# Projections and feed-forward products issued as four 32-column tiles

## The chip, the cores and the metric

The kernel runs on one core of a Trainium2 chip. The metric is the device time of one launch in microseconds. The page of the profile shows one execution of the program, taken by the hardware profiler; the times are those of separate runs.

## The reference

One layer of a graph transformer on x of shape (8, 2048, 256) in float32, with a 2048 x 2048 adjacency matrix as mask. F = 8 frames, N = 2048 rows, C = 256 channels, H = 8 heads of D = 32.

```
q, k, v = split(x @ w_qkv)                        # (F, N, 256) each, 8 heads of 32
attn    = softmax(where(adj > 0, q k^T / sqrt(32), -1e9))
x1      = layernorm(x + attn v) * g1 + be1
f       = relu(x1 @ w1 + b1) @ w2 + b2
x2      = layernorm(x1 + f) * g2 + be2
out     = layernorm(x + x2)
```

## The kernel before

All products are in float32. The main loop of `fast_path` runs over 1024 **items** (f, qc, g, mb): 8 frames, 4 chunks `qc` of 512 query rows, 2 groups `g` of 4 heads, 16 blocks `mb` of 128 key rows. Sixteen items with the same (f, qc, g) make one group of sums. An item does this:

- `scores` (L217, on TensorE, PE in the profile): four products k^T q, one per head, each from 32 partitions (contraction over 32 channels) to 128 rows by 512 columns. They use four row strips of the array side by side. They are issued two items ahead of their use (`LEAD = 2`), into three pairs of PSUM banks that rotate.
- L220 on VectorE (DVE) adds the mask to two heads at a time, from PSUM into an SBUF tile `p`; two of these per item.
- `exponentials` (L224 on ScalarE, ACT): one exponential over the four heads, 128 x 2048.
- `values` (L236): four products, one per head, v of 128 x 32 (stationary) with `p` of 128 x 512 (moving), each to 32 of the 128 PSUM partitions. They use four column strips of the array side by side.
- `add_up`: softmax denominators. The `p` tiles of sixteen items are summed partly by GpSimd (POOL, L258), partly by accumulating DMAs that GpSimd issues (L255).

Everything else is **fill**: generators that are advanced once per item, just ahead of the item's scores, by `advance`. Each has a due time. A generator yields `BANK` when it needs one of the two side PSUM banks, and at most one gets one per item; `MORE` splits a piece of PE work over two items where nothing else is late. So on PE the order is: values of item t, then one piece of fill (or none), then scores of item t+3, values of item t+1, and so on. The fill pieces on PE are:

- L174 in `channels`: a projection to q^T or k^T, two products (halves `a` of the 256 input channels) of a 128 x 128 weight block with x^T, 512 columns.
- L199 in `project`: the projection to v, 4 row blocks `j` times 2 halves `a`, x^T of 128 x 128 stationary, 128 columns of weights moving.
- L409 in `feed_forward`: as L174, with w1.
- L421 in `feed_forward`: 4 row blocks times 2 halves, h^T of 128 x 128 stationary, w2 of 256 columns moving.
- L294 in `denominator`: column sums with a 128 x 32 block of ones, four heads side by side in column strips, as the values.
- Transposes L151, L301, L330, L396, and L126 for the mask in the opening (`begin`).

ScalarE copies most of these pieces out of PSUM (L176, L202, L410); VectorE adds the output of L421 (L423), and takes the statistics of the norms (L265, L266). GpSimd finishes the norms and multiplies and adds the affine rows (L341, L343, L399, L401).

A float32 product appears in the trace as two weight loads (PEld, LDWEIGHTS) and two MATMUL records, so a piece of L174 with both halves, which is four records, is split by `MORE` into two pieces of two where it can be. The names PEld, PE, DVE, ACT, POOL and SP are those of the profile.

Of the kernel before, what the change touches and what calls it, by code (L numbers as in the profile page):

```python
# [19 lines left out]
P = 128  # L20
H = 8
D = 32
# [17 lines left out]
def stats(nc, small, t, mhalf):  # L40
    st = small.tile([P, nc.vector.BN_STATS_DIM], F32, name="st")
    nc.vector.bn_stats(st, t)
    mv = small.tile([P, nc.vector.BN_AGGR_DIM], F32, name="mv")
    nc.vector.bn_aggr(mv, st)
    rs = small.tile([P, 1], F32, name="rs")
    nc.gpsimd.tensor_scalar(rs, mv[:, 1:2], EPS, 1.0, op0=ALU.add, op1=ALU.mult)
    nc.gpsimd.tensor_tensor(rs, rs, mhalf, ALU.pow)
    return mv, rs


def normalize(nc, dst, t, mv, rs):
# [4 lines left out]
def fast_path(ctx, tc, cst, x, adj, out, RS):  # L56
    nc = tc.nc
    F, N, C = x.shape
# [20 lines left out]
    ident, identb, wqkv, w1s, w2s = cst["ident"], cst["identb"], cst["wqkv"], cst["w1s"], cst["w2s"]  # L79
# [7 lines left out]
    def bank(dt=F32):  # L87
        shape = [P, CH] if dt == F32 else [P, 2, CH]
        if state["side"] is not None:
            i = 1 - state["side"]  # L90
            return ps_x[i].tile(shape, dt, name=f"x{i}")
        i = state["turn"]
        state["turn"] = (i + 1) % 5
        pool = ps_s[i] if i < 3 else ps_x[i - 3]
        return pool.tile(shape, dt, name=f"s{i}" if i < 3 else f"x{i - 3}")
# [9 lines left out]
    def give(t):  # L105
        live[:] = [None if u is t else u for u in live]
# [35 lines left out]
    def queries(f, c, xT):  # L142
        for g in range(2):
            yield from channels(QT, qp, "qT", (f, c, g), xT, g * P)
# [23 lines left out]
    def channels(store, pool, name, key, xT, k0):  # L168
        yield BANK
        ps = bank()  # L170
        for a in range(2):
            if a:
                yield MORE
            nc.tensor.matmul(ps, wqkv[:, a, k0:k0 + P], xT[:, a, :], start=(a == 0), stop=(a == 1))  # L174
        store[key] = pool.tile([P, CH], F32, name=name)
        nc.scalar.copy(store[key], ps)  # L176

    def reload(f, c):
        while (f, c) not in XT:
            yield 1  # L180
        yield INPUTS - 1
        xT = take([P, 2, CH], F32)
        nc.sync.dma_start(xT, XD[f][c])
        yield 3
        return xT

    def project(f, c, g, xT=None):
        if xT is None:
            xT = yield from reload(f, c)
            while len(KT) < (2 * f + g) * NCK + c:  # L190
                yield 1
        yield from channels(KT, kp, "kT", (f, c, g), xT, C + g * P)
        yield BANK
        ps = bank()
        for j in range(TPC):
            if j == TPC // 2:
                yield MORE
            for a in range(2):
                nc.tensor.matmul(ps[:, j * P:(j + 1) * P], xT[:, a, j * P:(j + 1) * P],  # L199
                                 wqkv[:, a, 2 * C + g * P:2 * C + (g + 1) * P], start=(a == 0), stop=(a == 1))  # L200
        v = vp.tile([P, TPC, P], F32, name="v")
        nc.scalar.copy(v, ps.rearrange("p (j c) -> p j c", c=P))  # L202
        V[f, c, g] = v
        give(xT)
# [74 lines left out]
    def rows(v):  # L279
        return v[:, None, :].to_broadcast([P, TPC, C])  # L280
# [54 lines left out]
    def tail(f, qc, y, xin):  # L335
        yield from norm(y)
        yield from feed_forward(y)
        yield 1
        z = y
        yield from norm(z)  # L340
        nc.gpsimd.tensor_tensor(z, z, rows(cst["g2r"]), ALU.mult)  # L341
        yield 1
        nc.gpsimd.tensor_tensor(z, z, rows(cst["be2r"]), ALU.add)  # L343
        yield 1
        nc.gpsimd.dma_start(z, xin, accum_op=ALU.add)
        yield 7
        yield from norm(z)
        nc.sync.dma_start(out[f, qc * CH:(qc + 1) * CH, :].rearrange("(p j) c -> p j c", p=P), z)
        state["tails"] -= 1
# [20 lines left out]
    def finish(f, qc):  # L370
        y = yp.tile([P, TPC, C], F32, name="y")
        xr, xb = state["rows"], take([P, TPC, C], F32)
        yield from divide(f, qc, y)
        nc.vector.tensor_tensor(y, y, xr, ALU.add)
        norm_halves(y)
        nc.vector.tensor_tensor(xb, xr, rows(cst["be2r"]), ALU.add)
        yield from feed_forward(y)
        z = y
        norm_halves(z)
        for h in range(0, TPC, 2):  # L380
            nc.vector.tensor_tensor(z[:, h:h + 2], z[:, h:h + 2], rows(cst["g2r"])[:, h:h + 2], ALU.mult)
            nc.vector.tensor_tensor(z[:, h:h + 2], z[:, h:h + 2], xb[:, h:h + 2], ALU.add)
        norm_halves(z)
        dst = out[f, qc * CH:(qc + 1) * CH, :].rearrange("(p j) c -> p j c", p=P)
        for h in range(0, TPC, 2):
            nc.sync.dma_start(dst[:, h:h + 2], z[:, h:h + 2])

    def feed_forward(y):
        yield TURNED
        state["turned"] = True  # L390
        yT = work.tile([P, 2, CH], F32, name="turned")
        for a in range(2):
            yield BANK
            ps = bank()
            for j in range(TPC):
                nc.tensor.transpose(ps[:, j * P:(j + 1) * P], y[:, j, a * P:(a + 1) * P], ident)  # L396
            nc.scalar.activation(yT[:, a, :], ps, AF.Identity, bias=cst["be1c"][:, a:a + 1], scale=cst["g1c"][:, a:a + 1])
        yield 1
        nc.gpsimd.tensor_tensor(y, y, rows(cst["g1r"]), ALU.mult)  # L399
        yield 1  # L400
        nc.gpsimd.tensor_tensor(y, y, rows(cst["be1b2r"]), ALU.add)  # L401
        hT = work.tile([P, 2, CH], F32, name="hT")
        for d in range(2):
            yield BANK
            ps = bank()
            for a in range(2):
                if a:
                    yield MORE
                nc.tensor.matmul(ps, w1s[:, a, d * P:(d + 1) * P], yT[:, a, :], start=(a == 0), stop=(a == 1))  # L409
            nc.scalar.activation(hT[:, d, :], ps, AF.Relu, bias=cst["b1s"][:, d:d + 1], scale=1.0)  # L410
        state["turned"] = False
        yield 1
        z = y
        for jj in range(0, TPC, 2):
            yield BANK
            ps = bank()
            for j in range(jj, jj + 2):
                if j > jj:
                    yield MORE
                for d in range(2):  # L420
                    nc.tensor.matmul(ps[:, (j - jj) * C:(j - jj + 1) * C], hT[:, d, j * P:(j + 1) * P], w2s[:, d, :],  # L421
                                     start=(d == 0), stop=(d == 1))
            nc.vector.tensor_tensor(z[:, jj:jj + 2, :], ps.rearrange("p (b c) -> p b c", c=C), z[:, jj:jj + 2, :], ALU.add)  # L423


# [18 lines left out]
    def advance(t, free=True, finish=False):  # L444
# [18 lines left out]
        while state["holder"] and (finish or late and state["holder"][2] == MORE):  # L463
# [4 lines left out]


    NEXT = {(1, 1): [(turn, 0)], (3, 1): [(turn, 1)], (3, 10): [(project, 0, 0)], (5, 1): [(turn, 2)],  # L470
            (5, 8): [(project, 1, 0)], (6, 0): [(turn, 3)], (6, 4): [(project, 2, 0)], (6, 8): [(project, 3, 0)],
            (6, 12): [(project, 0, 1)], (7, 0): [(project, 1, 1)], (7, 4): [(project, 2, 1)], (7, 8): [(project, 3, 1)]}

    def begin():
# [91 lines left out]
def general_path(ctx, tc, cst, x, adj, out):  # L566
# [20 lines left out]
    with tc.For_i(0, F, 1) as f:  # L587
# [24 lines left out]
        with tc.For_i(0, N, P) as n0:  # L612
# [12 lines left out]
            for h in range(H):  # L625
# [27 lines left out]
                nc.vector.tensor_scalar(y[:, h * D:(h + 1) * D], o, rsum, None, op0=ALU.mult)  # L653
            nc.vector.tensor_tensor(y, y, xs, ALU.add)
            mv, rs = stats(nc, small, y, cst["mhalf"][:, 0:1])
            normalize(nc, y, y, mv, rs)
            nc.vector.tensor_tensor(y, y, cst["g1r"], ALU.mult)
# [17 lines left out]
            nc.vector.tensor_tensor(z, pf, y, ALU.add)  # L675
            nc.vector.tensor_tensor(z, z, cst["b2r"], ALU.add)
            mv, rs = stats(nc, small, z, cst["mhalf"][:, 0:1])
            normalize(nc, z, z, mv, rs)
            nc.vector.tensor_tensor(z, z, cst["g2r"], ALU.mult)
            nc.vector.tensor_tensor(z, z, cst["be2r"], ALU.add)  # L680
            nc.vector.tensor_tensor(z, z, xs, ALU.add)
            mv, rs = stats(nc, small, z, cst["mhalf"][:, 0:1])
            normalize(nc, z, z, mv, rs)
            nc.sync.dma_start(out[bass.ds(f, 1), bass.ds(n0, P), :].rearrange("o p c -> p (o c)"), z)
# [114 lines left out]
```

## Time and profile before

| | |
|---|---|
| median of 3 runs | 3441.08 us (3438.21 to 3442.04) |
| profiled execution, first to last instruction (span) | 3433.5 us |
| median less span | 7.6 us |
| PE busy | 3205.3 us, 22036 MATMUL records |
| DVE busy | 2736.9 us |
| ACT busy | 2427.4 us |
| POOL busy | 2588.2 us |
| DMA engines, 800 to 1300 us | busy 0.76 of the time |
| granted TensorE clock, mean | 0.985 |

The page gives the span of the profiled execution and what its engines did in it; its time as the runs are timed is not given, and the 7.6 us between the two rows is taken as what lies around the span. Busy time is the union of an engine's instructions, the mean of a group is that of one record, and records overlap on PE, where several products stream side by side. The start times of PE's records are what is read below: the distance from the first record of a piece to the first record of the next is what the piece costs.

### The profile page before, as it was taken

How to read it: one execution, taken by the hardware profiler on the slowest of the kernel's cores; microseconds unless marked ns; L12 is line 12 of the kernel's file. 1: busy time of each engine (PE TensorE's matmuls, PEld its weight loads, DVE VectorE, ACT ScalarE, POOL GpSimd, SP SyncE). 2: the span in 40 equal slices, each digit the busy share in tenths (PEclk: the TensorE clock that was granted, in tenths of full speed). 3: DMA queues.
4: the chain of work that ended last, by engine and by line, in shares of the span. 5: the costliest groups of instructions: out<-in, count | busy, mean ns of one | idle time of the engine just before them, and what ended most of it. 6: DMA issues, size and time to landing. Idle time of an engine off the chain costs nothing. (4 is left out here: it accounts for less than half of the span.)

```text
span 3433.5 us, 54404 instructions
## 1 busy us (share of the span) xinstructions
PE 3205.3 (93%) x22036; PEld 1035.0 (30%) x22036; DVE 2736.9 (80%) x3203; ACT 2427.4 (71%) x1937; POOL 2588.2 (75%) x1357
## 2 busy tenths in 40 slices
PE   7999999999999999999999999999999999999994
PEld 5222333223332333322332223322233223332222
DVE  4788877878778877888778788787878878788884
ACT  3677777767777767777767677777777767777773
POOL 0577778787777787888777787777777877787884
PEclk8999999999999999999999999999999999999997
DMA  8677778778678777778767778678787677777773
GB/s 308 149 158 166 180 167 185 149 153 198 151 171 171 161 169 176 160 164 184 174 151 173 158 165 193 147 160 174 165 184 164 149 170 178 169 168 154 153 154 85
DMA packets 149297, 575.98 MB, mean 168 GB/s; under 512 B 14608, under 2 KB 67344, under 8 KB 99888
## 3 DMA queue, kind: packets, MB, share of 16 engines
q0 software_dynamic: 64560, 435.85, 63.0%
q1 hardware_dynamic: 83664, 135.30, 11.7%
q8 instruction: 174, 2.85, 0.3%
q10 hardware_dynamic: 816, 1.31, 0.1%
q14 instruction: 83, 0.68, 0.1%
HBM read 131.99 MB, written 37.75 MB: 49 GB/s over the span
## 5 line engine op out<-in xcount | busy, mean ns | idle before, releaser
L220 DVE TENSOR_TENSOR p<-s,mask 128x1024 f32<-128x1024 f32 x2048 | 2409.3, 1218 | 561.6 <-PE s L217 326.4
L224 ACT ACTIVATE p<-p 128x2048 f32<-128x2048 f32 x1024 | 1956.0, 1910 | 535.4 <-DVE p L220 448.2
L258 POOL TENSOR_TENSOR p<-p 128x2048 f32<-128x2048 f32 x382 | 1815.1, 4755 | 311.1 <-ACT p L224 309.7
L217 PE MATMUL s<-qT,kT 32*128 32x512 f32 x8192 | 1174.4, 643 | 135.1 <-DVE p L220 129.6
L236 PE MATMUL x<-p,v 128*32 128x512 f32 x8192 | 1095.1, 607 | 2.4 <-ACT p L224 2.4
L255 POOL DMA_DIRECT2D p<-p x384 | 358.4, 989 | 426.0 <-DMA p<-p 201.6
L217 PEld LDWEIGHTS s<-qT,kT 32*128 32x128 f32 x8192 | 321.2, 183 | 741.8 <-DVE p L220 683.1
L236 PEld LDWEIGHTS x<-p,v 128*32 128x32 f32 x8192 | 161.4, 108 | 783.6 <-issue 282.1
L174 PE MATMUL x<-in,wqkv 128*128 128x512 f32 x472 | 257.3, 643 | 21.0 <-DMA in<-xd 17.2
L294 PE MATMUL x<-p,ones 128*32 128x512 f32 x2016 | 239.3, 592 | 0.0
L276 ACT ACTIVATE y<-y,nb,rs 128x256 f32<-128x256 f32 x372 | 219.3, 591 | 25.3 <-POOL nb L273 25.2
L265 DVE BATCH_NORM_STATS2 st<-y 128x6 f32<-128x256 f32 x372 | 154.9, 416 | 6.0 <-DMA y<-in_x_dram 6.0
L174 PEld LDWEIGHTS x<-in,wqkv 128*128 128x128 f32 x472 | 75.0, 191 | 206.1 <-issue 157.5
L421 PE MATMUL x<-w2s,hT 128*128 128x256 f32 x512 | 128.0, 392 | 0.0
L409 PE MATMUL x<-turned,w1s 128*128 128x512 f32 x248 | 127.3, 625 | 0.3 <-ACT hT L410 0.3
L296 ACT COPY dT<-x 128x512 f32<-128x512 f32 x63 | 36.9, 585 | 126.1 <-PE x L294 126.1
L199 PEld LDWEIGHTS x<-wqkv,in 128*128 128x128 f32 x896 | 105.8, 191 | 64.6 <-issue 35.2
L199 PE MATMUL x<-wqkv,in 128*128 128x128 f32 x896 | 120.5, 284 | 0.0
L421 PEld LDWEIGHTS x<-w2s,hT 128*128 128x128 f32 x512 | 91.9, 189 | 64.1 <-issue 50.8
L294 PEld LDWEIGHTS x<-p,ones 128*32 128x32 f32 x2016 | 65.5, 110 | 150.8 <-issue 150.2
L270 POOL TENSOR_TENSOR rs<-rs,mhalf 128x4 f32<-128x4 f32 x93 | 97.1, 1044 | 7.7
L176 ACT COPY kT<-x 128x512 f32<-128x512 f32 x59 | 34.5, 585 | 81.0 <-PE x L174 81.0
(117 smaller groups left out, 1433.5 us busy)
## 6 DMA issues: line engine op xcount, KB each, us to landing
p<-p POOLq DMA_DIRECT2D x384, 1024.0 KB, 10.4
mask<-md SPq DMA_DIRECT2D x248, 128.0 KB, 6.8
y<-in_x_dram POOLq DMA_DIRECT2D x62, 512.0 KB, 5.8
in<-xd SPq DMA_DIRECT2D x59, 512.0 KB, 10.2
p<-in_adj_dram SPq DMA_DIRECT2D x16, 1024.0 KB, 10.0
out_dram<-y SPq DMA_DIRECT2D x31, 512.0 KB, 3.0
in<-in_x_dram SPq DMA_DIRECT2D x29, 512.0 KB, 10.0
xd<-in SPq DMA_DIRECT2D x28, 512.0 KB, 7.6
```

Of the source, the lines that this page charges most:

```text
L174: nc.tensor.matmul(ps, wqkv[:, a, k0:k0 + P], xT[:, a, :], start=(a == 0), stop=(a == 1))
L199: nc.tensor.matmul(ps[:, j * P:(j + 1) * P], xT[:, a, j * P:(j + 1) * P], wqkv[:, a, 2 * C + g * P:2 * C + (g + 1) * P], start=(a == 0), s ...
L217: nc.tensor.matmul(ps2[half][:, j, :], KT[f, mb // TPC, g][r:r + D, (mb % TPC) * P:(mb % TPC + 1) * P], QT[f, qc, g][r:r + D, :], start=Tr ...
L220: nc.vector.tensor_tensor(pt[:, 2 * half:2 * half + 2, :], ps, MK[f, qc, mb // 2][:, mb % 2, None, :].to_broadcast([P, 2, CH]), ALU.add)
L224: nc.scalar.activation(PT[item], PT[item], AF.Exp, scale=1.0 / math.sqrt(D))
L236: nc.tensor.matmul(O[grp][r:r + D, :], V[f, mb // TPC, g][:, mb % TPC, r:r + D], PT[item][:, h, :], start=(mb == 0), stop=(mb == LAST))
L255: nc.gpsimd.dma_start(PT[f, qc, g, chain[0]], PT.pop(item), accum_op=ALU.add)
L258: nc.gpsimd.tensor_tensor(first, first, PT.pop(item), ALU.add)
L265: nc.vector.bn_stats(st, t[:, j, :])
L276: nc.scalar.activation(t[:, j, :], t[:, j, :], AF.Identity, bias=nb[:, j:j + 1], scale=rs[:, j:j + 1])
L294: nc.tensor.matmul(ps[r:r + D, :], cst["ones"], term[:, h, :], start=(n == 0), stop=(n == len(terms) - 1))
L421: nc.tensor.matmul(ps[:, (j - jj) * C:(j - jj + 1) * C], hT[:, d, j * P:(j + 1) * P], w2s[:, d, :], start=(d == 0), stop=(d == 1))
```

## The change

A new helper issues one product as four, each with 32 columns of the stationary operand, to 32 of the output's partitions. The four products L174, L199, L409 and L421 go through it. Nothing else changes: the loops, the banks, the yields, the copies and the queues are as before, and no operand is laid out anew. The number of PE records for these four lines goes up fourfold. All lines below the helper move down by five.

```diff
+def in_columns(nc, out, lhsT, rhs, start, stop):
+    for r in range(0, P, D):
+        nc.tensor.matmul(out[r:r + D], lhsT[:, r:r + D], rhs, start=start, stop=stop)

 # channels
-            nc.tensor.matmul(ps, wqkv[:, a, k0:k0 + P], xT[:, a, :], start=(a == 0), stop=(a == 1))
+            in_columns(nc, ps, wqkv[:, a, k0:k0 + P], xT[:, a, :], start=(a == 0), stop=(a == 1))

 # project
-                nc.tensor.matmul(ps[:, j * P:(j + 1) * P], xT[:, a, j * P:(j + 1) * P],
-                                 wqkv[:, a, 2 * C + g * P:2 * C + (g + 1) * P], start=(a == 0), stop=(a == 1))
+                in_columns(nc, ps[:, j * P:(j + 1) * P], xT[:, a, j * P:(j + 1) * P],
+                           wqkv[:, a, 2 * C + g * P:2 * C + (g + 1) * P], start=(a == 0), stop=(a == 1))

 # feed_forward
-                nc.tensor.matmul(ps, w1s[:, a, d * P:(d + 1) * P], yT[:, a, :], start=(a == 0), stop=(a == 1))
+                in_columns(nc, ps, w1s[:, a, d * P:(d + 1) * P], yT[:, a, :], start=(a == 0), stop=(a == 1))
...
-                    nc.tensor.matmul(ps[:, (j - jj) * C:(j - jj + 1) * C], hT[:, d, j * P:(j + 1) * P], w2s[:, d, :],
-                                     start=(d == 0), stop=(d == 1))
+                    in_columns(nc, ps[:, (j - jj) * C:(j - jj + 1) * C], hT[:, d, j * P:(j + 1) * P], w2s[:, d, :],
+                               start=(d == 0), stop=(d == 1))
```

## The prediction

> **What bounds the kernel now.** First the busy shares of the page:
>
> ```profile
> PE 3205.3 (93%) x22036; PEld 1035.0 (30%) x22036; DVE 2736.9 (80%) x3203; ACT 2427.4 (71%) x1937; POOL 2588.2 (75%) x1357
> ```
>
> PE leads, but busy time on PE is modelled, so I read the distances between starts instead, in the timeline of PE. Two stretches of it (start, length, engine, line, tiles, count, and in brackets the idle time before it):
>
> ```profile
> 730.63 1.16 PE L199 MATMUL x<-wqkv,in 128*128 128x128 f32 x8
> 731.72 1.14 PE L217 MATMUL s<-qT,kT 32*128 32x512 f32 x8
> 732.79 1.06 PE L236 MATMUL x<-p,v 128*32 128x512 f32 x8
> ...
> 739.91 1.14 PE L217 MATMUL s<-qT,kT 32*128 32x512 f32 x8 [0.41 <-DVE p L220]
> 740.98 1.07 PE L236 MATMUL x<-p,v 128*32 128x512 f32 x8
> 742.45 1.14 PE L217 MATMUL s<-qT,kT 32*128 32x512 f32 x8 [0.41 <-DVE p L220]
> ```
> ```profile
> 800.80 1.06 PE L236 MATMUL x<-p,v 128*32 128x512 f32 x8
> 801.80 1.98 PE L409 MATMUL x<-turned,w1s 128*128 128x512 f32 x4
> 803.71 1.14 PE L217 MATMUL s<-qT,kT 32*128 32x512 f32 x8
> 804.78 1.06 PE L236 MATMUL x<-p,v 128*32 128x512 f32 x8
> 805.78 1.99 PE L421 MATMUL x<-w2s,hT 128*128 128x256 f32 x8
> 807.70 1.14 PE L217 MATMUL s<-qT,kT 32*128 32x512 f32 x8
> ...
> 812.76 1.07 PE L236 MATMUL x<-p,v 128*32 128x512 f32 x8
> 813.64 1.90 PE L294 MATMUL x<-p,ones 128*32 128x512 f32 x16
> 815.48 1.14 PE L217 MATMUL s<-qT,kT 32*128 32x512 f32 x8
> ```
>
> An item without fill takes 2.54 us (739.91 to 742.45): PE needs 2.07 and then waits 0.41 for the mask add of DVE, which has 2 x 1.22 us to do. DVE bounds it. An item with a piece of fill takes 3.1 us or more, with no wait on PE: PE bounds it. So a gain in the fill counts, as long as the item stays longer than DVE's and ACT's work in it. The list of waits says the same, with little waiting on PE in all:
>
> ```profile
> PE s L217 <- DVE p L220: 129.6, 276, 1.4
> PE x L174 <- DMA in<-xd: 17.2, 7, 3.4
> ```
>
> [...] Values to scores, or to any full-array piece, take 996 ns from start to start (median, all lines); values to L294, which has the values' tile shape, take 882. The drain is 114 ns. [...] after a change of mode, the second record of a full-array product starts 533 to 534 ns after the first and that of the values 454, which over 427 of streaming leaves 107 and 27. Inside one mode the load is hidden: two more records of L174 cost 858 ns (1914 less 1056). [...] Here four pairs of load and product start 6.7 ns apart. [...]
>
> **The change, piece by piece.** VectorE, ScalarE, GpSimd and the DMA queues keep their instructions and (bar a few at the end) their order; on PE no piece moves. L174, L199, L409 and L421 stream the same columns, in the values' mode instead of the full-array mode.
>
> Each piece follows values and precedes scores. Before: values 996 (with the drain), then the piece with its exposed load and drain. After: values 882, then the piece's stream, then a drain of 114 before the scores, as L294 shows it: 1830 for 16 records, 2 x 858 + 114.
>
> - L174, L409, 2 records: before 996 + 1056 = 2052. After 882 + 858 + 114 = 1854. **198 ns** less. With 4 records 858 more on both sides, so 198 again.
> - L199, 8 records: before 996 + 1088 = 2084; a record streams in 111.6 ns ((1981 - 1088) / 8). After 882 + 893 + 114 = 1889. **195 ns** less.
> - L421, 4 records: before 996 + 1060; 864 for four more. After 882 + 864 + 114. **196 ns** less.
>
> In the timeline of PE I count the periods from values to values with one of these: 191 of L174, 78 of L409, 77 of L199, 63 of L421. 269 x 0.198 + 140 x 0.195 = **80.6 us** off PE, all in items that PE bounds now.
>
> Not all of it reaches the end. In each of the 409 periods I took DVE's and ACT's busy time, plus 30 ns per instruction for the gap between two; the period cannot fall below either. Many periods of L174 hold norm statistics (0.42 + 0.18 us) besides the two mask adds, 3.03 us of DVE in a period of 3.12, so little is won there. Item by item 57 us are left (54 with a gap of 60 ns, 66 with none). Averaged over three items, where a late DVE catches up in the next, 72. I take 58: scores run only three half-items ahead, so little is lent, and POOL lends nothing (below).
>
> In the opening the pieces L174 and L199 stand between transposes, all in one mode now. Eight chunks get two changes of mode each: 114 + 27 into the strips, 114 + 107 back, 0.36 us a chunk, 2.9 us in all. PE runs without a gap from 36 to 55 us there, but afterwards waits for DVE's conversion of the adjacency matrix. I take 1.5 on the path; 0 and 2.9 are the ends.
>
> The new cost that the trace of before does not show is four times the records per streamed column: 8 (four loads, four products) for each 111.6 ns of L199, 14 ns a record; 27 ns for L421, 54 for L174 and L409, as in the values and L294 today. Can they be supplied? Two readings. A burst after a wait comes at 6.7 ns a pair. And at the start of the kernel the queue is empty:
>
> ```profile
> 7.68 1.56 PEld L151 LDWEIGHTS s<-ident,p 128*128 128x128 f32 x8 [7.68 <-POOL ident masks.py:199]
> 7.71 1.94 PE L151 MATMUL s<-ident,p 128*128 128x128 f32 x8 [7.71 <-DMA p<-in_x_dram]
> ...
> 9.47 1.22 PE L174 MATMUL s<-p,wqkv 128*128 128x512 f32 x1
> ```
>
> The sequencer's own semaphore wait for L174, which is queued behind these 16 records, is recorded at 7.741, 136 ns after the one ahead of them (7.605). So 16 records passed in at most 136 ns, 8.5 each. That is under 14, and the sequencer otherwise runs 24 records ahead. I cost it at nothing; what hides it is the stream of the piece itself. Upper end: rival D.
>
> Sum: -58 + 1.5 = -56.5, on a profiled span of 3433.5 (to 3377); with the 7.6 us around it, against the median of 3441.08: **3384.6**, say 3384.
>
> **The rivals.** About 0.2% (7 us) is what a measurement of this kernel can tell from no change.
>
> A. As summed: 3384, from 3354 (all 80.6, and L199's records at 107 instead of 111.6: 4.7 more) to 3396. Chance 0.60.
>
> B. POOL takes over. It is busy 390 of 500 us in mid-kernel, and waits 202 us in all for its accumulating DMAs; together 84% of the span. In the chain that ended last, 3115 to 3176 us is all POOL and DMA, and PE waited 1.06 us at 3168. In its favour: a late POOL delays the norm's `nb`, then ACT in order, then the exponentials. Against: earlier frames have 102 us for two groups of 16 items where the last has 95. With 0.5 to 1 us lost in each of 32 pairs of groups the gain falls to 25 to 41: 3400 to 3416. Chance 0.13.
>
> C. The strips' loads are not hidden in short records: 27 ns for each of 1024 records of L199 and 512 of L421, 41 us on PE, half the gain. Or the strips of a piece do not join the values' mode and the drain stays (409 x 0.114 = 47 us on PE, so the change does only half of what it says). At the same ratio of path to PE (57 of 80.6) that leaves 24 to 28: 3413 to 3417. Against: L294 after values shows neither, but at 427 ns a record. Chance 0.12.
>
> D. Slower: issue. Place: L199, where the records are densest. [...] 31 ns a record (31 is also what lies between the load and its product when PE restarts after a sequencer wait, at 1516.42). A piece then takes 64 x 31 = 1984 instead of 893, 128 pieces 140 us, less 24 records of lead (0.74 us) in each of 77 periods, 57: 82 us added, and after the 57 saved elsewhere 25 more than before, 3466. It decides from about 27 ns a record. [...] Against: the 8.5 ns above. Chance 0.12.
>
> The remaining 0.03: gains and losses within the 0.2%.
>
> **How the numbers follow.** Faster by over 0.2%: A, B, C, 0.84. Within: 0.04. Slower: D, 0.12. The range leaves out D and a little of the rest: 3354 to 3428, the upper end a bad C with the whole opening cost.
>
> **What would show it.** Right: values to the next piece 882 instead of 996 ns; L174's piece 972 instead of 1056, L199's 1007 instead of 1088; more waiting of scores on L220 than 129.6 us; DVE, ACT and POOL busy times unchanged. Records of L199's strips more than 112 ns apart per group of four mean C or D: D if all records are evenly 27 ns or more apart and PE runs out of work in L199, C if four start together and the next four late. Values still 996 ahead of these pieces would mean that they don't share a mode. POOL's waits shrinking while PE's waits grow mean B.

## The result and the profile after

The changed kernel takes 3393.32 us (median of 4 runs, 3390.63 to 3399.32) against 3441.56 (4 runs), a ratio of 0.9868 with a 95% interval of 0.985 to 0.9885: 48 us less. The forecast was 57 less. The profiled execution has a span of 3397.4 us and a time of 3399.32; only 1.9 us lie around a span, so the profile of before (span 3433.5) shows a run that was some 6 us faster than the median, that of after one 6 us slower. The two spans differ by 36 us, the medians by 48.

All lines below the helper are five higher, and the four products are now on line 53. The busy shares of the page after:

```profile
PE 3133.4 (92%) x28948; PEld 978.7 (29%) x28948; DVE 2736.3 (81%) x3203; ACT 2431.0 (72%) x1937; POOL 2595.8 (76%) x1357
```

6912 more records on PE, and 72 us less of PE busy. The other engines do what they did. The timeline of PE, at pieces that answer to those shown of before (start, length, engine, line, tiles, count, and idle time before):

```profile
729.25 1.07 PE L241 MATMUL x<-p,v 128*32 128x512 f32 x8
730.14 1.05 PE L53 MATMUL x<-wqkv,in 128*32 128x128 f32 x32
731.12 1.14 PE L222 MATMUL s<-qT,kT 32*128 32x512 f32 x8
...
786.62 1.06 PE L241 MATMUL x<-p,v 128*32 128x512 f32 x8
787.50 1.04 PE L53 MATMUL x<-in,wqkv 128*32 128x512 f32 x8
788.47 1.14 PE L222 MATMUL s<-qT,kT 32*128 32x512 f32 x8
789.54 1.07 PE L241 MATMUL x<-p,v 128*32 128x512 f32 x8
790.42 1.90 PE L53 MATMUL x<-turned,w1s 128*32 128x512 f32 x16
792.25 1.14 PE L222 MATMUL s<-qT,kT 32*128 32x512 f32 x8
794.50 1.07 PE L241 MATMUL x<-p,v 128*32 128x512 f32 x8 [1.10 <-ACT p L229]
```

From the start of the values to the start of the piece there are now 0.88 to 0.89 us instead of 1.00. A piece of one projection product takes 0.97 instead of 1.06, and eight records of the v projection, now 32, take 0.98 instead of 1.09. All is as forecast, the last a little better: over all pieces of L199 the median is 986 ns where 1007 were expected, and for double pieces 1860 where 1900 were. From single to double piece, 128 columns in four strips take 109 ns ((1860 - 986) / 8) and not 111.6. What the prediction calls the drain is the 114 ns between 996 and 882, and its mode is the tile shape of the records: the traces show between which shapes the starts lie 114 ns further apart, not what the array does meanwhile. The load is measured: in the trace of before the first two loads of L174 at 1505.04 start 108 ns apart (128 columns), the first two of the values on one strip at 1500.92 start 28 apart (32 columns), and the second record of each starts 427 behind its load. The sum off PE is 269 x 198 + 63 x 196 + 42 x 216 + 35 x 235 ns = 83 us.

The last line shows where some of it went: the values wait 1.10 us for the exponential, which they hardly did before. Three lists of waits of the kernel after (who waited for whom: us in total, times, longest; parts of the lists), of PE, ACT and POOL:

```profile
PE s L222 <- DVE p L225: 127.6, 270, 1.4
PE x L53 <- DMA in<-xd: 29.0, 8, 7.2
PE x L241 <- ACT p L229: 23.7, 20, 3.9
```
```profile
ACT y L281 <- POOL nb L278: 61.8, 20, 9.4
```
```profile
POOL p L260 <- DMA p<-p: 241.2, 63, 8.1
POOL p L263 <- ACT p L229: 240.2, 79, 88.3
```

The same waits before, of the values, of ScalarE on `nb` and of GpSimd on its DMAs (for the scores and the reloads see the prediction: 129.6 and 17.2):

```profile
PE x L236 <- ACT p L224: 2.4, 2, 2.1
ACT y L276 <- POOL nb L273: 25.2, 14, 9.1
POOL p L255 <- DMA p<-p: 201.6, 50, 7.8
```

The waiting of the scores on VectorE has not grown at all, which speaks against a clip by VectorE; the runs without the DMA adds, below, test it. From the first values to the last the two profiles differ by 40.8 us of the 83, so 42 are missing (outside of this stretch the profile of after is another 4.7 us longer). PE's waits on reloads, exponentials and `hT` L415 grew by 11.8 + 21.3 + 5 = 38 us; others fell by 5, which leaves 33. The other 9 us are not waits: PE's own work took longer, most of it at long waits. The longest of them:

```profile
1498.12 1.07 PE L241 MATMUL x<-p,v 128*32 128x512 f32 x8
1506.43 1.94 PE L53 MATMUL x<-in,wqkv 128*32 128x512 f32 x8 [7.24 <-DMA in<-xd]
1508.29 1.93 PE L222 MATMUL s<-qT,kT 32*128 32x512 f32 x8
1510.15 1.07 PE L241 MATMUL x<-p,v 128*32 128x512 f32 x8
```

The piece and the scores behind this wait take 1.86 us each, where 0.97 and 1.07 are usual; from 1503.1 to 1509.9 us the granted clock is 0.50 in this trace. Against the median of their own kind, the pieces that touch such a stretch lost 19 us between the first and the last values, and 13 before. Behind the opening and up to the last values, each of these stretches lies at a wait of PE, of 2.41 to 7.24 us in the profile of after and of 2.77 to 3.77 us in that of before.

### The profile page after: what moved, and what is told of

Same layout as the page of the kernel before. It is cut to its first block, busy times and chain, and to the rows that moved or that the text cites. A ratio compares the mean times of both kernels' runs of the same rounds, so it can differ in the third digit from the quotient of the medians.

```text
span 3397.4 us, 68228 instructions
## 1 busy us (share of the span) xinstructions
PE 3133.4 (92%) x28948; PEld 978.7 (29%) x28948; DVE 2736.3 (81%) x3203; ACT 2431.0 (72%) x1937; POOL 2595.8 (76%) x1357
## 5 line engine op out<-in xcount | busy, mean ns | idle before, releaser
L225 DVE TENSOR_TENSOR p<-s,mask 128x1024 f32<-128x1024 f32 x2048 | 2410.1, 1218 | 530.6 <-PE s L222 331.6
L222 PE MATMUL s<-qT,kT 32*128 32x512 f32 x8192 | 1176.3, 644 | 133.2 <-DVE p L225 127.6
L241 PE MATMUL x<-p,v 128*32 128x512 f32 x8192 | 1096.8, 607 | 23.7 <-ACT p L229 23.7
L260 POOL DMA_DIRECT2D p<-p x384 | 364.3, 1016 | 443.7 <-DMA p<-p 241.2
L53 PE MATMUL x<-in,wqkv 128*32 128x512 f32 x1888 | 242.5, 603 | 29.9 <-DMA in<-xd 29.0
L281 ACT ACTIVATE y<-y,nb,rs 128x256 f32<-128x256 f32 x372 | 219.4, 591 | 61.8 <-POOL nb L278 61.8
L53 PE MATMUL x<-turned,w1s 128*32 128x512 f32 x992 | 123.2, 603 | 5.0 <-ACT hT L415 4.9
L53 PE MATMUL x<-w2s,hT 128*32 128x256 f32 x2048 | 123.8, 382 | 0.4 <-ACT hT L415 0.4
L53 PEld LDWEIGHTS x<-wqkv,in 128*32 128x32 f32 x3584 | 101.0, 110 | 46.1 <-issue 31.4
L53 PEld LDWEIGHTS x<-in,wqkv 128*32 128x32 f32 x1888 | 61.3, 111 | 176.0 <-issue 149.5
L53 PE MATMUL x<-wqkv,in 128*32 128x128 f32 x3584 | 111.9, 273 | 0.0
L53 PEld LDWEIGHTS x<-w2s,hT 128*32 128x32 f32 x2048 | 67.0, 111 | 73.2 <-issue 37.5
## 6 DMA issues: line engine op xcount, KB each, us to landing
p<-p POOLq DMA_DIRECT2D x384, 1024.0 KB, 10.4
```

The costliest lines, as they stand in the source:

```text
L53: nc.tensor.matmul(out[r:r + D], lhsT[:, r:r + D], rhs, start=start, stop=stop)
L222: nc.tensor.matmul(ps2[half][:, j, :], KT[f, mb // TPC, g][r:r + D, (mb % TPC) * P:(mb % TPC + 1) * P], QT[f, qc, g][r:r + D, :], start=Tr ...
L225: nc.vector.tensor_tensor(pt[:, 2 * half:2 * half + 2, :], ps, MK[f, qc, mb // 2][:, mb % 2, None, :].to_broadcast([P, 2, CH]), ALU.add)
L241: nc.tensor.matmul(O[grp][r:r + D, :], V[f, mb // TPC, g][:, mb % TPC, r:r + D], PT[item][:, h, :], start=(mb == 0), stop=(mb == LAST))
L260: nc.gpsimd.dma_start(PT[f, qc, g, chain[0]], PT.pop(item), accum_op=ALU.add)
L281: nc.scalar.activation(t[:, j, :], t[:, j, :], AF.Identity, bias=nb[:, j:j + 1], scale=rs[:, j:j + 1])
```

## The experiments

**Theory 1**: a strip piece saves the 114 ns between the values and the piece, and the difference between a load of 128 columns and one of 32 (107 and 27 ns in the trace of before), once per piece and whatever its columns; four strips have no issue cost. **Theory 2**: what PE gains and the end does not get is taken by GpSimd and its accumulating DMAs. Rivals: the short records gain by themselves; strips of any width stand 882 ns behind the values, not 996; VectorE and ScalarE clip the gain.

### One half of the change at a time

In each, the two other products call `nc.tensor.matmul` as before:

```diff
 # wide only
-                in_columns(nc, ps[:, j * P:(j + 1) * P], xT...      # L199, L421 of before
+                whole(nc, ps[:, j * P:(j + 1) * P], xT...
 # short only
-            in_columns(nc, ps, wqkv[:, a, k0:k0 + P], xT...         # L174, L409 of before
+            whole(nc, ps, wqkv[:, a, k0:k0 + P], xT...
```

> Only the 512-column products (projections to q and k, first feed-forward product) go in four strips; the short ones (128 and 256 columns) stay full-array. Theory (drain and exposed load are saved once per piece): 191 + 78 pieces at 198 ns, 53 us off PE, values to these pieces 882 ns, values to the short pieces 996 as before. On the time 31 us at the ratio of the whole change (48 of 83), at most 53: about 3410, not below 3388. Rival (the gain comes from the many short records that supply or load better in strips): these pieces give little, under 15 us.

Measured: 3413.31 us, ratio 0.9917 (0.9891 to 0.9943), 28 us less than the 3441.29 of before in this comparison. From the values to the wide pieces there are 883 ns (median), to the short ones 996; a wide piece of one product takes 972.

> Only the short products (projection to v, second feed-forward product) go in four strips. Theory: 42 x 216 + 35 x 235 + 63 x 196 ns = 30 us off PE; on the time 17 to 30: 3412 to 3424, and with the wide ones alone it adds up to the whole change. Rival (short records give the gain): 35 us or more here. Rival (only the sum is too fast for GpSimd and its DMAs, each part alone loses nothing): 53 and 30 us, more together than the whole change gives.

Measured: 3417.1 us, 0.9926 (0.9901 to 0.9952), 24 us less; values to the short pieces 883, to the wide ones 996. The halves give 28 + 24 = 52 where the whole gives 48, so they add up within what these runs can tell. Of 53 us off PE the wide half kept 28, so part of the loss is there with it alone. Of 30 the short half kept 24, but its interval, 17 to 34 us, includes all 30, so a loss there is not shown by the time. In both profiles ScalarE's wait on `nb` lies between before and after (46.6 and 47.1 us).

### Two strips of 64

```diff
-    for r in range(0, P, D):
-        nc.tensor.matmul(out[r:r + D], lhsT[:, r:r + D], rhs, start=start, stop=stop)
+    for r in range(0, P, 2 * D):
+        nc.tensor.matmul(out[r:r + 2 * D], lhsT[:, r:r + 2 * D], rhs, start=start, stop=stop)
```

> All four products in two strips of 64 columns instead of four of 32. Theory (strips save the drain only where they have the values' tile shape): values to a piece stays 996 ns; the exposed load shrinks from 107 to about 53 ns, so a piece of two records costs 1003 instead of 1056; 409 x 0.053 = 22 us off PE, 13 to 22 on the time: 3419 to 3428. Rival (any column strips join): values to a piece 882 and a piece near 972, as the 32-column kernel, 3393.

Measured: 3426.12 us, 0.9958 (0.9948 to 0.9969), 15 us less. The timeline of PE in this kernel:

```profile
387.19 1.06 PE L241 MATMUL x<-p,v 128*32 128x512 f32 x8
388.18 1.94 PE L53 MATMUL x<-turned,w1s 128*64 128x512 f32 x8
390.05 1.14 PE L222 MATMUL s<-qT,kT 32*128 32x512 f32 x8
```

From the values to the piece there are 0.99 us (median 996 ns), as with the full array: tiles of 128 x 64 next to tiles of 128 x 32 do not save the 114 ns. The piece of two products takes 1.87 where the full array took 1.91, and a piece of one 1009 ns (median) against 1056. The second record of a strip starts 480 ns after the first, where it was 533 in the full array. So the two parts of the saving come apart: the load of 64 columns gives some 50 of the 198 ns (533 less 480), and the 114 between values and piece come only with the shared tile shape.

### The opening left full-array

```diff
-            in_columns(nc, ps, wqkv[:, a, k0:k0 + P], xT...
+            (whole if state["side"] is None else in_columns)(nc, ps, wqkv[:, a, k0:k0 + P], xT...
...                                                              # the same at L199 of before
```

> As the changed kernel, but in the opening, where the pieces stand between transposes, they stay full-array. Theory: the first values product starts at about 96.0 us as before and not at 99.5, the loop is as in the changed kernel: 2 to 4 us less than 3393, so 3389 to 3391. Rival (the later start was a DMA that came late by chance): no difference to the changed kernel.

Measured: 3393.01 us, 0.9858 (0.9833 to 0.9884), the same as the changed kernel. The first values start at 99.28 us here, though the opening's pieces are full-array. In the profiles of this document they start between 96.0 and 101.2, with strips in the opening or without. The rival was right: the later start in the profile of after (99.5 against 96.0) can't be put down to the strips.

### Without the accumulating DMAs

These two kernels leave six of the sixteen exponential tiles of each group out of the denominators.

```diff
             if mb in chain[1:]:
-                nc.gpsimd.dma_start(PT[f, qc, g, chain[0]], PT.pop(item), accum_op=ALU.add)
+                PT.pop(item)
```

> The kernel before without the accumulating DMAs of the denominators: six of the sixteen exponential tiles of a group are left out of the sums, nothing else. This takes the DMA waits off GpSimd and its queue. Expected: somewhat faster than before, 3400 to 3435, since GpSimd's waits delay the norms here too (25 us of ScalarE idle on the norm's nb). It is the base for the next.

Measured: 3403.49 us (3402.28 to 3404.9), 0.9898 (0.9882 to 0.9915).

> The changed kernel without the accumulating DMAs of the denominators (the same six of sixteen tiles left out). Theory (the part of PE's gain that did not reach the end was taken by GpSimd, its accumulating DMAs and the reloads that share the DMA engines): the distance to the same edit of the kernel before is 70 to 83 us instead of 48. Rival (VectorE and ScalarE clip the gain item by item): the distance stays 45 to 58 us.

Measured: 3319.78 us (3319.18 to 3320.39), 0.9654 (0.9638 to 0.967). The distance between the two is 83.7 us, and 83 is what was counted off PE. In the profile of the second, the values to a piece take 883 ns in the mean and not only in the median, and of PE's waits none on a reload is left and 0.4 us on exponentials. ScalarE's wait on `nb` is down to this:

```profile
ACT y L281 <- POOL nb L278: 9.3, 1, 9.3
```

So VectorE and ScalarE let the whole gain through. Everything that was lost hangs on the accumulating DMAs. Their removal takes away GpSimd's waiting behind them and their traffic, and frees the `p` tiles earlier; the runs that follow take these apart in part.

### Normalising later

```diff
         nc.gpsimd.tensor_scalar(nb, nb, -1.0, 1.0, op0=ALU.mult, op1=ALU.mult)
-        yield 2
+        yield 4
```

> The kernel before with the normalisation on ScalarE issued two items later after the statistics (yield 4 instead of 2), so that a late GpSimd holds up no exponentials. Theory: at most 10 us faster than before (ScalarE idles 25 us there on the norm's nb). Rival (longer chains of tails cost more): slower by some us.

Measured: 3471.55 us, 1.0096 (1.0079 to 1.0113), 32 us slower.

> The changed kernel with the same later normalisation. Theory (a late GpSimd holds ScalarE, in order, ahead of the exponentials): ScalarE's idle time on nb falls from 62 us to under 20, the values wait for exponentials under 5 us instead of 24, and the time falls by 10 to 25 us below the changed kernel: 3368 to 3383. Rival (the stalls only move to the reloads and to the tiles that the accumulating DMAs release): the same 3393 within 5 us.

Measured: 3451.96 us, 1.0035 (1.0021 to 1.0049), 59 us slower than the changed kernel, outside of what either side expected. The wait aimed at did go: ScalarE's wait on `nb` fell from 61.8 to 16.7 us, and the values' wait on exponentials from 23.7 to 1.0. But the fill behind the norms moved too. PE's waiting on L225 rose from 127.6 to 187.8 us, and 419 items carry a piece of strips, not 409. Between the first and the last values the profile is 48 us longer than that of the changed kernel: 32 us are waits, and most of the rest is PE at a granted clock of 0.50, in 21 stretches instead of 8. The edit was no clean test of the stall, since it moves VectorE's work too, and it leaves open what the wait on `nb` alone costs.

### The same DMAs, further apart

The six DMA adds of a group form two chains, each adding into one tile, and GpSimd waits at an add until the one ahead of it in its chain has landed (241.2 us in the list of after; from issue to landing 10.4 us, median, in the profiles of before and after). What stands behind such an add in GpSimd's program starts behind it, a norm's `nb` too: in the trace of after the add at 1502.87 had waited 6.68 us for a DMA, and the `rs` of a norm whose statistics were done at 1498.67 starts at 1509.70, its last `nb` at 1511.38. Consecutive adds of a chain are mostly three items apart, which take 7.6 us without fill and some 9 with single pieces. The next edit makes it four.

```diff
-    POOLED = (0, 3, 6, 8, 11, 13, 15)
-    MOVED = ((1, 4, 7, 10), (2, 5, 9, 12))
-    ALONE = 14
-    ENDED = (13, 15)
+    POOLED = (0, 3, 5, 7, 9, 11, 13)
+    MOVED = ((1, 4, 8, 12), (2, 6, 10, 14))
+    ALONE = 15
+    ENDED = (11, 13)
```

> The changed kernel with the denominators' sums dealt out anew: POOLED 0, 3, 5, 7, 9, 11, 13, the two DMA chains 1, 4, 8, 12 and 2, 6, 10, 14, alone 15. The same number of GpSimd adds, DMA adds, bytes and PE terms; in a chain, consecutive DMA adds now stand four items apart instead of mostly three. Theory (GpSimd, in order, stands behind the preceding DMA of its chain, some 10.4 us against three items of 2.5 to 3.8 us): its wait on p<-p falls from 241 us to under 120, ScalarE's idle time on nb from 62 to under 35, and the time to 3365 to 3382. Rival (the DMA engines' bandwidth, not GpSimd's queue, takes the gain, through late reloads and tiles): 3393 within 6 us, with the reloads' waits of 29 us still there. Rival (the chain that ends at 14 comes too late for the denominator): slower than 3393.

Measured: 3326.77 us (3322.57 to 3330.1), 0.9677 (0.966 to 0.9694): 112 us less than before, 67 less than the changed kernel, with all of the traffic, and far below the 3365 to 3382 expected. It is the fastest kernel here whose denominators are whole. GpSimd's and ScalarE's waits in it, and the landing of the adds (KB each, median us from issue to landing), first in the changed kernel, then here:

```profile
POOL p L263 <- ACT p L229: 571.4, 170, 87.0
...
POOL p L260 <- DMA p<-p: 16.6, 10, 2.5
```
```profile
ACT y L281 <- POOL nb L278: 9.3, 1, 9.3
```
```profile
p<-p POOLq DMA_DIRECT2D x384, 1024.0 KB, 10.4
p<-p POOLq DMA_DIRECT2D x384, 1024.0 KB, 8.8
```

GpSimd now waits for exponentials, so it is ahead of its work, and hardly for its DMAs: 16.6 us instead of 241.2. The DMA engines were busier (0.80 between 800 and 1300 us, 0.78 in the changed kernel, 0.76 before), and the reloads' wait is out of the list. So it was the way in which the adds are dealt out, not their bytes. The new deal also moves GpSimd's own adds and the times at which `p` tiles come free, so how much of the 67 us belongs to the four items alone is not separated.

> The kernel before with the same new deal of the sums. Theory: its stalls were smaller (25 us of ScalarE on nb, 2 us of values on exponentials), so it gains less than the changed kernel does: 0 to 15 us, and the distance between the two spaced kernels grows from 48 towards 60 to 80. Rival (bandwidth): the distance stays at 45 to 52.

Measured: 3407.42 us, 0.9902 (0.9882 to 0.9922), 31 us less. That is more than expected: the stall was already dear before, though PE's list of waits then named only 20 us on reloads and exponentials. The distance between the two spaced kernels is 80.7 us, against 48 unspaced. That the unchanged kernel gains 31 us by the new deal also explains why the changed one gained so much more than expected: about 31 of its 67 us were there to be had before the change. With all their bytes, the spaced kernels lie only 7.0 and 3.9 us above those without any accumulating DMA (3326.77 and 3319.78, 3407.42 and 3403.49), so the traffic itself costs little here.

## Why the prediction was right, and where not

- **Change of shape and load per piece**: right to within a few ns for L174 and L409 (883 and 972) and L421 (1.84 us for a double piece, as expected). The saving of L199 was undersized by 21 to 40 ns a piece. 80.6 us were forecast, 83 counted. This also answers rival C: the values stand 883 ns ahead of these pieces and not 996, and the short records stream no slower than before.
- **The issue of four times as many records (rival D)**: costed at nothing, and nothing it was. L199 now sustains 8 records in 109 ns, 13.7 ns each, against the 27 from which it would have decided by the prediction's estimate. Its price of 31 ns a record was an estimate from one distance, that of a load to its product at 1516.42. The 8.5 ns read from the sequencer's wait at the start of the kernel was the reading that carried this.
- **The clip by VectorE and ScalarE item by item (80.6 to 58)**: this step failed, and the size of VectorE's work was its error. An item with norm statistics was put at 3.03 us of VectorE, the sum of its instructions' durations and 30 ns a gap (as between L265 and L266: 774.91 + 0.42 to 775.36). But these instructions overlap, and the trace of before shows what they take from start to start:

```profile
782.85 2.35 DVE L220 TENSOR_TENSOR p<-s,mask 128x1024 f32<-128x1024 f32 x2 [1.13 <-PE s L217]
785.12 0.42 DVE L265 BATCH_NORM_STATS2 st<-y 128x6 f32<-128x256 f32 x1
785.57 0.18 DVE L266 BATCH_NORM_AGGREGATE mv<-st 128x2 f32<-128x6 f32 x1
785.68 2.35 DVE L220 TENSOR_TENSOR p<-s,mask 128x1024 f32<-128x1024 f32 x2
```

  From mask add to mask add, with the statistics between, there are 2.83 us (785.68 - 782.85). That fits into the new period of 2.93 us, so nothing had to be clipped. With overlaps counted once and no gaps, the same item-by-item sum gives 77 of the 80.6 us. Between the two spaced kernels all 191 periods of L174 are shorter by at least 196 ns, and 77 of the 78 of L409. More waiting of scores on VectorE was forecast, and it fell from 129.6 to 127.6 us. A first sign was there: averaged over three items the estimate was already 72.
- **Rival B**: this is what took the clip's place. The chain that it described is in the waits (GpSimd late on its DMAs, `nb` late, ScalarE in order, exponentials late, values waiting). In the trace of after ScalarE waits 3.31 us for `nb`, up to 382.31, the exponential behind it in ScalarE's program starts at 382.82, though its mask adds ended at 378.99, and the values wait 1.56 us for it, up to 384.77. The last of these waits all but go with the new deal (values 23.7 to 0.4 us). It did not name the reloads (12 us more waiting) nor the slower PE behind long waits (6 us more). Its price was 0.5 to 1 us in each of 32 pairs of groups, 16 to 32 us; measured are 35 (83 less 48), 1.1 us a pair. The sum of A put this stall at nothing. The prediction took 84% of GpSimd's time, busy and waiting together, as leaving room; but its waits were the stall, and already cost 31 us before. What it did not see was their cause, the way in which the adds are dealt out (most likely their distance in a chain, see above).
- **The number**: 57 less against 48 less. That it came so near is luck: two errors, a clip that did not occur (23 us) and a stall that A counted at nothing (35 us), nearly cancel.
- **The opening** (1.5 us on the path): not resolved by these runs. **The 7.6 us around the span**: wrong, it is 1.9; the rest was the scatter of the profiled run.

## What to carry to other kernels

Where pieces of different tile shapes alternate on PE, price the change of shape from starts to starts between neighbours of equal and of unequal shape; giving a full-size product its neighbour's shape cost nothing in streaming here and saved 0.2 us a piece. When one engine is relieved, price what another needs per item from start to start too: durations added up made an item of VectorE's work 0.2 us longer than it is. And follow the chain of issues on the queues that work in order (here GpSimd, which waited 241.2 us for its own DMAs): waits on its own transfers are not room. Last, test with the suspected stall taken out of both kernels: the distance of 84 us beside 48 answered at once what averages could not.

## What the runs showed of the hardware

From the values, which are 128 x 32, to strips of 128 x 64 the starts lay 996 ns apart, as to the full array; to strips of 128 x 32 they lay 883 apart (882 to L294 before). So the 114 ns went with the same tile shape, not with strips of any width. A second float32 product of 512 columns took 858 ns in four strips of 32 (1830 less 972) as in the full array (1914 less 1056), and in the pieces with 128 columns the strips sustained 13.7 ns a record, loads and products counted alike. The longest wait of PE in the trace of after cost more than its 7.24 us: from 1503.1 to 1509.9 the granted clock was 0.50, and the piece behind the wait took 1.86 us instead of 0.97.

Before ranged over 21 us (3430.06 to 3451.17 in 20 runs), and without the accumulating DMAs four runs lay within 1.2 us (3319.18 to 3320.39). That the scatter hangs on these DMAs is not shown: four runs of the kernel before with the later norm, which has them all, lay within 1.9 us.
